# Seven products for eight in the MLP of a two-layer cross-attention kernel, with the last half's finished quarter stored first

## The chip, the core and the metric

The kernel runs on one core of one Trainium2 chip. The metric is the device time of one execution in microseconds (us), as a median over runs. All data are 4-byte floats. A core has TensorE (PE: matmuls, with its weight loads shown as PEld), VectorE (DVE), ScalarE (ACT), GpSimd (POOL) and SyncE (SP), which here only issues transfers. Each engine works through its own queue in order, and semaphores tie the queues together.

## The reference

Inputs are `x` (8 batches, 100 queries, 512 features) and a context (8, 361, 512). A first small cross-attention adds to `x`. Then comes one decoder layer with two cross-attentions of 16 heads of 128 (the context is key and value of both) and an MLP with 2048 hidden values. The change concerns the MLP alone:

```python
h = _layer_norm(x, ln_mlp_scale, ln_mlp_offset)
h = jax.nn.gelu(h @ w_fc1 + b_fc1, approximate=False) @ w_fc2 + b_fc2
return x + h
```

With 800 queries it is a product 800 x 512 x 2048 and one of 800 x 2048 x 512.

## The kernel before

Activations stand transposed: features on the 128 partitions, queries along the free dimension. The MLP is done in two halves (`hf` 0 and 1) of four batches, 400 queries each. A half has these units, built by `mlp_units`:

- `norm`: eight units `normed(2, q, c)` that normalise (L536) and transpose (`ph`, L542) into `hT`, 4 chunks of 128 features by 400 queries (L545).
- `hid`: sixteen units `hidden(hf, f)`, one for each 128 hidden values: four matmuls of 128x400 into one PSUM tile `pg` (L895), summed over the four feature chunks, and a Gelu with bias on ScalarE (L898) into `g`. The first eight go to a tile of their own, the others to a piece of the big constant tile `Z`, free by then.
- `mlp`: four units `mlp_out(hf, c)`, one for each 128 outputs: sixteen matmuls of 128x400 into `pf` (L907) over the hidden chunks, and an Identity with bias (L908) into `ys`, another piece of `Z`.
- `end`: four units `back`, one for each batch: four transposes into `pb` (L878), an add to the residual `xs` on VectorE (L879) and the store to `out` on the SP queue (L911).

Weights arrive through a ring of six slots of 512 KB (`W_SLOTS`, `Ring`). `emit` walks the list of units in order; when the last use of a tile is emitted, the fetch of the tile six places on is emitted too, on SP (L140). The framework adds the semaphores: a fetch waits for the last reader of its slot. The first layer's tiles hold 512 features by 256 hidden values, the second's 1024 hidden values by 128 outputs.

The order of the units is written out by hand at the end of the kernel; `woven` spreads one list over another. The framework's scheduler may then move an instruction a few places within its engine's queue. The last part of the order is:

```python
units += held[9:] + norm[:4] + woven(drain, norm[4:])
units += hid + woven(mlp, norm1) + woven(hid1, end) + mlp1 + end1
```

`drain` is the rest of the last attention, with its output projection `pwo` (L871: matmuls of 128x200). So in time: first half's hidden values, its outputs among the second half's transposes, second half's hidden values among the first half's ends, second half's outputs, its ends.

Other parts of the kernel already form seven products in place of eight: blocks of scores (`pair_part`, with sums from `pair_sums` on GpSimd, L668 to L671) and of probabilities times context (`mixed`, L795, with sums from `column_sums` on GpSimd, L759 to L762). There a partial result is copied or added out of a PSUM bank while the bank goes on accumulating, so that three banks `x`, `y`, `z` make four output blocks. In the first attention, `ctx_transposed` forms sums on VectorE (L423 to L425) while `ctx_sums` does so on GpSimd (L398 to L402).

Of the kernel before, what the change touches and what calls it, by code (L numbers as in the profile page):

```python
# [9 lines left out]
F32 = mybir.dt.float32  # L10
AF = mybir.ActivationFunctionType
ALU = mybir.AluOpType
# [27 lines left out]
B11, B21, B22, T1, T2, T3, T4 = range(7)  # L40


A11, A12, A22, A13, A23, A33, M1, M2, M3, M4 = range(10)
# [36 lines left out]
def two_cross_attentions(ctx: ExitStack, tc: tile.TileContext, a: dict, out: bass.AP):  # L80
    nc = tc.nc
# [11 lines left out]
    def psum(pool, shape, name):  # L93
        return pool.tile(shape, F32, tag=pool.name, name=name)
# [81 lines left out]
    def w4(key):  # L176
        return rings["w"].tiles[key].rearrange("p (c n) -> p c n", c=DT)

    def w8(key):
        return rings["w"].tiles[key].rearrange("p (h n) -> p h n", h=8)  # L180
# [5 lines left out]
    units = []  # L186

    def unit(fn, *keys):
        return fn, keys

    def emit():
        for _, keys in units:
            for ring, key in keys:
                rings[ring].plan(key)
        for ring in rings.values():
            ring.issue()
        for fn, keys in units:
            fn()
            for ring, key in keys:
                rings[ring].used(key)  # L200
                rings[ring].issue()
# [5 lines left out]
    zf = Z.rearrange("p c b r -> p (c b r)")  # L207
# [39 lines left out]
    vec_b = const.tile([P, len(VB), DT], F32, tag="vec_b", name="vec_b")  # L247
    vec = {v: vecs[:, i, :] for i, v in enumerate(VA + VC)}
# [7 lines left out]
    half = const.tile([L, 1], F32, tag="half", name="half")  # L256
# [264 lines left out]
    hTs = {}  # L521

    def normed(n, q, c):
        if c == 0:
            if n < 2:
                hTs[n, q] = work.tile([P, DT, NQ], F32, tag="hT", name=f"hT_{n}_{q}", bufs=1)
            elif q % 2 == 0:
                t = cpool.tile([P, 7 * 2 * KH], F32, tag="cT", name=f"hT_{n}_{q}")
                t = t[:, : DT * 2 * NQ].rearrange("p (c n) -> p c n", c=DT)
                for i in range(2):  # L530
                    hTs[n, q + i] = t[:, :, i * NQ : (i + 1) * NQ]
                hTs["mlp", q // 2] = t
            for j in range(QB):
                b = q * QB + j
                h = work.tile([L, D], F32, tag="h", name=f"h_{n}_{b}")
                nc.vector.tensor_scalar(  # L536
                    h, xs[b], mv[:, b, 0:1], rstd[:, b : b + 1], ALU.subtract, ALU.mult
                )
                hTs["rows", j] = h
        pt = psum(ps_t, [P, NQ], f"ph_{n}_{q}_{c}")  # L540
        for j in range(QB):
            nc.tensor.transpose(  # L542
                pt[:, j * L : (j + 1) * L], hTs["rows", j][:, c * P : (c + 1) * P], ident[:L, :L]
            )
        nc.vector.tensor_scalar(  # L545
            hTs[n, q][:, c, :], pt, vec_b[:, 2 * n, c : c + 1], vec_b[:, 2 * n + 1, c : c + 1], ALU.mult, ALU.add
        )
# [101 lines left out]
    pTs, probs, sums = {}, {}, {}  # L649
# [213 lines left out]
    ys = {}  # L863
# [7 lines left out]
            nc.tensor.matmul(ps, w[:, h % 8, :], oTs[l, q][:, h, :], start=(h == 0), stop=(h == H - 1))  # L871
        nc.scalar.activation(ys[l, q][:, c, :], ps, AF.Identity, bias=vec_b[:, 6 + l, c : c + 1])

    def back(y, off, b, then):

        ps = psum(ps_t, [L, D], f"pb_{b}")
        for c in range(DT):
            nc.tensor.transpose(ps[:, c * P : (c + 1) * P], y[:, c, off : off + L], ident)  # L878
        nc.vector.tensor_tensor(xs[b], ps, xs[b], ALU.add)  # L879
        then(b)  # L880


    gs = {}

    def hidden(hf, f):
        if f % 8 == 0:
            if f == 0:
                t = opool.tile([P, 8, 2 * NQ], F32, tag="o", name=f"g_{hf}_{f}")
            else:
                t = zf[:, (2 + hf) * 3200 : (3 + hf) * 3200].rearrange("p (f t) -> p f t", f=8)  # L890
            gs[hf, f // 8] = t
        w = w4(("f1", hf, f // 2))
        ps = psum(ps_mm, [P, 2 * NQ], f"pg_{hf}_{f}")
        for c in range(DT):
            nc.tensor.matmul(  # L895
                ps, w[:, c, (f % 2) * P : (f % 2 + 1) * P], hTs["mlp", hf][:, c, :], start=(c == 0), stop=(c == DT - 1)
            )
        nc.scalar.activation(gs[hf, f // 8][:, f % 8, :], ps, AF.Gelu, bias=vec["b_fc1"][:, f : f + 1])  # L898

    def mlp_out(hf, c):  # L900
        if c == 0:
            n = DT * 2 * NQ
            ys["mlp", hf] = zf[:, hf * n : (hf + 1) * n].rearrange("p (c t) -> p c t", c=DT)
        ps = psum(ps_mm, [P, 2 * NQ], f"pf_{hf}_{c}")
        for f in range(16):
            w = w8(("f2", hf, c, f // 8))
            nc.tensor.matmul(ps, w[:, f % 8, :], gs[hf, f // 8][:, f % 8, :], start=(f == 0), stop=(f == 15))  # L907
        nc.scalar.activation(ys["mlp", hf][:, c, :], ps, AF.Identity, bias=vec_b[:, 8, c : c + 1])  # L908

    def store(b):  # L910
        nc.sync.dma_start(out=out[b], in_=xs[b])  # L911
# [2 lines left out]
    W = "w"  # L914
# [41 lines left out]
    def close_units(l, q):  # L956
        res = [
            unit(lambda c=c: attn_out(l, q, c), (W, ("wo", l, q, c, 0)), (W, ("wo", l, q, c, 1)))
            for c in range(DT)
        ]  # L960
        res += [unit(lambda j=j: back(ys[l, q], j * L, q * QB + j, ln_stats)) for j in range(QB)]
        return res

    def mlp_units(hf):
        norm = [unit(lambda q=q, c=c: normed(2, q, c)) for q in (2 * hf, 2 * hf + 1) for c in range(DT)]
        hid = [unit(lambda f=f: hidden(hf, f), (W, ("f1", hf, f // 2))) for f in range(F // P)]
        mlp = [
            unit(lambda c=c: mlp_out(hf, c), (W, ("f2", hf, c, 0)), (W, ("f2", hf, c, 1))) for c in range(DT)
        ]
        end = [unit(lambda j=j: back(ys["mlp", hf], j * L, hf * 4 + j, store)) for j in range(4)]  # L970
        return norm, hid, mlp, end

    def woven(x, y):

        if not x:
            return y
        res, k = [], 0
        for n, u in enumerate(x):
            res.append(u)
            upto = (n + 1) * len(y) // len(x)  # L980
            res += y[k:upto]
            k = upto
        return res
# [37 lines left out]
    for n, (l, q, g) in enumerate(steps):  # L1021
        ahead = project_units(n + 1) if n + 1 < len(steps) else []
        half_ahead = (len(ahead) + 1) // 2
        for j in range(QB):
            fill = []
            if j == 0 and n and g == 1 and (l, q) != (0, 0):
                pl, pq, _ = steps[n - 2]
                fill += close_units(pl, pq)
            mix = mix_units(n, 0) if j else mix_units(n - 1, 1) if n else []
            part = ahead[:half_ahead] if j == 0 else ahead[half_ahead:]  # L1030
# [7 lines left out]
            part = woven(part, outs) if len(part) > len(outs) else woven(outs, part)  # L1038
            if mix:
                lead = (len(part) + 2) // 3 if ahead else len(part) - 2 + j  # L1040
                fill += part[:lead]
                part = part[lead:]
# [3 lines left out]
            if l == 0 and q == 1:  # L1046
                k = 2 * g + j
                fill += e_units(1)[4 * k // 3 : 4 * (k + 1) // 3]
            groups = score_units(n, j)
            k = 0  # L1050
            for i, us in enumerate(groups):
# [3 lines left out]
                k = upto  # L1055
    n = len(steps) - 1
    drain = mix_units(n, 1) + out_units(n) + close_units(1, B // QB - 1)
    norm, hid, mlp, end = mlp_units(0)
    norm1, hid1, mlp1, end1 = mlp_units(1)
    units += held[9:] + norm[:4] + woven(drain, norm[4:])  # L1060
    units += hid + woven(mlp, norm1) + woven(hid1, end) + mlp1 + end1
    emit()


# [23 lines left out]
```

## Time and profile before

| | us |
|---|---|
| median of 3 runs | 2073.28 (2072.14 to 2075.76) |
| the profiled execution | 2074.07 |
| its span | 2072.3 |
| TensorE busy (share of the span) | 2014.7 (97%) |
| VectorE, ScalarE, GpSimd busy | 1165.6, 748.5, 575.7 |
| pg (L895), first half | 1888 to 1931 |
| pf (L907), first half, with the second half's transposes | 1931 to 1975.5 |
| pg, second half, with the first half's ends | 1975.5 to 2020.3 |
| pf, second half | 2020.3 to 2063.3 |
| from there to the end of the span | 9.0 |

The span is the program on the chip in the profile; the time of an execution has some 1.8 us more around it. "Busy" is the union of an engine's instructions. The profile shows a 4-byte matmul as two records, each with a weight load of its own; their ends are modelled and overlap the next record, so the distance between starts says what one costs. Slices are fortieths of the span, 51.8 us each. The chain of waits is followed back from the last instruction, at each step to what released it.

### The profile page before, as it was taken

Reading aid. Unit: us, or ns where it says so; the run is one execution under the profiler, and the core shown is the slowest. Engines: PE = TensorE matmul, PEld = TensorE weight load, DVE = VectorE, ACT = ScalarE, POOL = GpSimd, SP = SyncE. Lnnn points to the kernel's source line nnn. Section 1 sums busy time; section 2 is a strip of 40 time slices with the busy share of each in tenths; the row PEclk is TensorE's granted clock in tenths of the full one; section 3 lists DMA queues with packets and bytes.
Section 4 is the critical chain, followed back from the end, with each engine's and each line's share of the span. In section 5 each row is a group of like instructions: output and inputs, shape, how many; then the busy total and the mean of one; then the engine's idle time right before and its main releaser. Section 6 shows DMA issues by size and latency. Waiting matters only on the chain. (4 is left out here: it accounts for less than half of the span.)

```text
span 2072.3 us, 30186 instructions
## 1 busy us (share of the span) xinstructions
PE 2014.7 (97%) x10735; PEld 1770.9 (85%) x10735; DVE 1165.6 (56%) x3363; ACT 748.5 (36%) x1962; POOL 575.7 (28%) x1042
## 2 busy tenths in 40 slices
PE   9989999999999999999999999999999999989998
PEld 5768899898899989998998999989998999877554
DVE  2564776657764766476645766476647574750000
ACT  1224544434343444244433443344334442421110
POOL 3332442323242234223232333233322322310000
PEclk9999999999999999999999999999999999999999
DMA  8784235442444134414442344234332433113331
GB/s 259 261 300 133 89 85 177 124 150 81 133 147 144 65 103 147 142 45 134 154 145 93 103 137 126 93 89 149 109 111 77 153 105 115 50 54 123 100 103 50
DMA packets 254109, 256.87 MB, mean 124 GB/s; under 512 B 35756, under 2 KB 226640, under 8 KB 250632
## 3 DMA queue, kind: packets, MB, share of 16 engines
q1 hardware_dynamic: 249776, 244.58, 37.0%
q0 software_dynamic: 2112, 6.40, 0.9%
q10 hardware_dynamic: 2072, 3.97, 0.6%
q8 instruction: 85, 1.39, 0.3%
q14 instruction: 64, 0.52, 0.1%
HBM read 229.24 MB, written 25.67 MB: 123 GB/s over the span
## 5 line engine op out<-in xcount | busy, mean ns | idle before, releaser
L331 DVE STREAM_TRANSPOSE pT<-p 32x192 f32<-32x192 f32 (+1 forms) x1664 | 602.2, 362 | 85.0 <-ACT p L315 57.1
L795 PE MATMUL mx<-pT,ctx 128*128 128x256 f32 (+3 forms) x960 | 282.7, 393 | 12.9 <-DVE Z L821 5.5
L685 PE MATMUL sx<-cT,Z 128*128 128x181 f32 x1152 | 229.4, 318 | 4.8 <-DVE p L725 4.8
L795 PE MATMUL mz<-pT,ctx 105*128 105x256 f32 (+3 forms) x768 | 209.8, 396 | 11.2 <-POOL pT L759 9.4
L685 PEld LDWEIGHTS sx<-cT,Z 128*128 128x128 f32 x1152 | 195.7, 191 | 18.5 <-DVE p L725 6.8
L795 PEld LDWEIGHTS mx<-pT,ctx 128*128 128x128 f32 (+1 forms) x960 | 169.9, 190 | 35.4 <-POOL pT L761 8.0
L641 PE MATMUL pqw<-q,wkT 128*128 128x200 f32 x1024 | 195.8, 333 | 0.0
L625 PE MATMUL pq<-hT,wq 128*128 128x200 f32 x1024 | 194.0, 333 | 1.7 <-DMA wq<-in_L_xattn_wq_dram 1.7
L847 PE MATMUL po<-Z,wv 128*128 128x200 f32 x1024 | 193.9, 333 | 0.6 <-DMA wv<-in_L_xattn_wv_dram 0.6
L795 PEld LDWEIGHTS mz<-pT,ctx 128*128 128x128 f32 (+1 forms) x768 | 145.4, 193 | 46.0 <-POOL pT L759 12.8
L641 PEld LDWEIGHTS pqw<-q,wkT 128*128 128x128 f32 x1024 | 177.2, 190 | 5.4 <-ACT p L315 0.3
L625 PEld LDWEIGHTS pq<-hT,wq 128*128 128x128 f32 x1024 | 175.0, 189 | 7.4 <-issue 2.0
L719 POOL TENSOR_SCALAR p<-nsb 128x1 f32<-128x1 f32 x192 | 33.3, 193 | 526.3 <-DVE pT L331 481.8
L847 PEld LDWEIGHTS po<-Z,wv 128*128 128x128 f32 x1024 | 174.8, 189 | 5.2 <-issue 1.6
L739 ACT ACTIVATE p<-p,nm 128x362 f32<-128x362 f32 x192 | 114.8, 598 | 169.2 <-DVE nm L738 167.5
L871 PE MATMUL pwo<-oT,wo 128*128 128x200 f32 x1024 | 175.8, 332 | 0.0
L871 PEld LDWEIGHTS pwo<-oT,wo 128*128 128x128 f32 x1024 | 173.2, 190 | 0.0
L668 POOL TENSOR_TENSOR sums<-Z 128x256 f32<-128x256 f32 x96 | 69.9, 728 | 324.2 <-ACT Z L644 188.8
L738 DVE TENSOR_REDUCE nm<-p 128x1 f32<-128x362 f32 x192 | 101.5, 529 | 99.0 <-ACT p L730 87.4
L685 PE MATMUL sz<-cT,sums 128*128 128x181 f32 x768 | 150.6, 318 | 0.4 <-ACT p L713 0.4
L644 ACT COPY Z<-pqw 128x400 f32<-128x400 f32 x256 | 122.9, 489 | 74.3 <-PE pqw L641 74.1
L315 ACT ACTIVATE p<-p,rden 128x362 f32<-128x362 f32 (+2 forms) x216 | 129.6, 600 | 31.0 <-DVE rden L314 30.9
(310 smaller groups left out, 2720.7 us busy)
## 6 DMA issues: line engine op xcount, KB each, us to landing
wv<-in_L_xattn_wv_dram SPq DMA_DIRECT2D x64, 512.0 KB
wq<-in_L_xattn_wq_dram SPq DMA_DIRECT2D x64, 512.0 KB
wo<-in_L_xattn_wo_dram SPq DMA_DIRECT2D x64, 512.0 KB
wkT<-wkd SPq DMA_DIRECT2D x48, 512.0 KB
cT<-cTd SPq DMA_DIRECT2D x16, 1267.0 KB
f<-in_L_xattn_w_fc_dram SPq DMA_DIRECT2D x32, 512.0 KB
wkr<-in_L_xattn_wk_dram SPq DMA_DIRECT2D x16, 512.0 KB
ctx<-cxd SPq DMA_DIRECT2D x16, 512.0 KB
```

Of the source, the lines that this page charges most:

```text
L315: nc.scalar.mul(p[:rows, :n], p[:rows, :n], rden[:rows])
L331: nc.vector.transpose(dst[keys, :, :, i, :], src[i * QD : (i + 1) * QD, :, :, quarter, :])
L625: nc.tensor.matmul(ps, w[:, c, (h % 2) * K : (h % 2 + 1) * K], hTs[l, q][:, c, :], start=(c == 0), stop=(c == DT - 1),)
L641: nc.tensor.matmul(ps[:, c, :], w[:, h % 2, cc * P : (cc + 1) * P], qs[h], start=True, stop=True)
L644: nc.scalar.copy(Z[:, 2 * c2 : 2 * c2 + 2, :, h * L : (h + 1) * L], ps.rearrange("p c (b t) -> p c b t", b=QB),)
L668: nc.gpsimd.tensor_tensor(t[:, 0], a2[:, :2, :], a2[:, 2:, :], ALU.add)
L685: nc.tensor.matmul(ps[:, :KH], st["a"][a][:, c, :], st["ct"][:, blk, c, :], start=(first and c == 0), stop=(c == 1), skip_group_check=not ...
L738: nc.vector.tensor_reduce(nm, p[:, :S1], AX.X, ALU.max, negate=True)
L739: nc.scalar.activation(p[:, :S1], p[:, :S1], AF.Exp, bias=nm, accum_out=den)
L795: nc.tensor.matmul(ps, cx[:w, blk, :], pT[:w, u, :], start=first, stop=last, skip_group_check=more)
L847: nc.tensor.matmul(ps, w[:, c, (h % 2) * K : (h % 2 + 1) * K], Z[:, c, :, h * L : (h + 1) * L], start=(c == 0), stop=(c == DT - 1),)
L871: nc.tensor.matmul(ps, w[:, h % 8, :], oTs[l, q][:, h, :], start=(h == 0), stop=(h == H - 1))
```

## The change

Both MLP products are done in blocks: outputs in two rows of blocks, inputs (the contraction) in two, and the 400 queries in two columns of 200 (a quarter of all queries each). Four output blocks then take seven block products in place of eight. Sums of weight blocks (S1, S2, S3, S4) and of value blocks (T1 to T4) are formed first; S3 and T3 replace a block in place.

- `hidden_in` forms the input's T sums on VectorE. `hidden_sums` forms the first layer's weight sums for a block of 256 hidden values from each of two tiles (`k` and `4 + k`) on GpSimd. `hidden` has four parts per block; its seven products are four matmuls of 128x200 each. Results are copied out on ScalarE, completed by an add on VectorE, and given their Gelu in place (A22 T4's directly from PSUM). At the end of a block VectorE forms the T sums of the hidden values.
- `mlp_sums` forms the second layer's weight sums for two outputs chunks (`c`, `c + 2`) on VectorE, and `mlp_out` has four parts with seven products of eight matmuls of 128x200.
- `left_sums` and `right_sums` are the sums' formulas. `g`'s second tile and the T sums now have one place in `Z` for both halves, where each half had its own.
- `back` can do its transposes in two goes. The batches `j` = 2 and 3 of a half, whose outputs lie in the blocks c12 and c22, end first; in the second half they are put inside the last product (`between`, after its fourth matmul), and of batches 0 and 1 three transposes stand ahead of the last.
- Weights are fetched in the new order of use; a tile pair is held for the whole of its block.

```diff
@@ -871,41 +871,145 @@
             nc.tensor.matmul(ps, w[:, h % 8, :], oTs[l, q][:, h, :], start=(h == 0), stop=(h == H - 1))
         nc.scalar.activation(ys[l, q][:, c, :], ps, AF.Identity, bias=vec_b[:, 6 + l, c : c + 1])
-    def back(y, off, b, then):
-
-        ps = psum(ps_t, [L, D], f"pb_{b}")
-        for c in range(DT):
+    pbacks = {}
+    def back(y, off, b, then, chunks=range(DT)):
+        if b not in pbacks:
+            pbacks[b] = psum(ps_t, [L, D], f"pb_{b}")
+        ps = pbacks[b]
+        for c in chunks:
             nc.tensor.transpose(ps[:, c * P : (c + 1) * P], y[:, c, off : off + L], ident)
+        if DT - 1 not in chunks:
+            return
+        del pbacks[b]
         nc.vector.tensor_tensor(xs[b], ps, xs[b], ALU.add)
         then(b)
...
+    gs, ts, ws, mm = {}, {}, {}, {}
+    def right_sums(engine, b11, b12, b21, b22, t1, t2, t4):
+        engine.tensor_tensor(t1, b12, b11, ALU.subtract)
+        engine.tensor_tensor(t2, b22, t1, ALU.subtract)
+        engine.tensor_tensor(b12, b12, b22, ALU.subtract)
+        engine.tensor_tensor(t4, b21, t2, ALU.subtract)
+    def left_sums(engine, a11, a12, a21, a22, s1, s2, s4):
+        engine.tensor_tensor(s1, a21, a22, ALU.add)
+        engine.tensor_tensor(s2, s1, a11, ALU.subtract)
+        engine.tensor_tensor(s4, a12, s2, ALU.subtract)
+        engine.tensor_tensor(a21, a21, a11, ALU.subtract)
+    def blocks_of(t, n):
+        return [t[:, i * n : (i + 1) * n, j * NQ : (j + 1) * NQ] for i in range(2) for j in range(2)]
+    def hidden_in(hf):
+        h = blocks_of(hTs["mlp", hf], 2)
+        t = work.tile([P, 3, 2, NQ], F32, tag="pb", name=f"ht_{hf}", bufs=1)
+        right_sums(nc.vector, *h, t[:, 0], t[:, 1], t[:, 2])
+        ts["h", hf] = dict(zip(("B11", "T3", "B21", "B22", "T1", "T2", "T4"), h + [t[:, i] for i in range(3)]))
+        g0 = opool.tile([P, 8, 2 * NQ], F32, tag="o", name=f"g_{hf}")
+        g1 = zf[:, 3200:6400].rearrange("p (f t) -> p f t", f=8)
+        t = zf[:, 6400:11200].rearrange("p (u f t) -> p u f t", u=3, f=8)
+        g = [x[:, :, j * NQ : (j + 1) * NQ] for x in (g0, g1) for j in range(2)]
+        gs[hf] = g
+        ts["g", hf] = dict(zip(("B11", "T3", "B21", "B22", "T1", "T2", "T4"), g + [t[:, i] for i in range(3)]))
+    def hidden_sums(hf, k):
+        w1, w2 = w4(("f1", hf, k)), w4(("f1", hf, 4 + k))
+        t = work.tile([P, 3, 2, 256], F32, tag="pT", name=f"fs_{hf}_{k}")
+        blocks = [w1[:, :2], w1[:, 2:], w2[:, :2], w2[:, 2:]]
+        left_sums(nc.gpsimd, *blocks, t[:, 0], t[:, 1], t[:, 2])
+        ws["h", hf, k] = dict(zip(("A11", "A12", "S3", "A22", "S1", "S2", "S4"), blocks + [t[:, i] for i in range(3)]))
+    def hidden(hf, k, part):
+        a, b = ws["h", hf, k], ts["h", hf]
+        c11, c12, c21, c22 = (g[:, 2 * k : 2 * k + 2, :] for g in gs[hf])
+        key = "h", hf, k
+        def add(name, sa, sb, first=False):
+            if first:
+                mm[key, name] = psum(ps_mm, [P, 2, NQ], f"p{name}_{hf}_{k}")
+            ps = mm[key, name]
+            for f in range(2):
+                for c in range(2):
+                    nc.tensor.matmul(
+                        ps[:, f, :], a[sa][:, c, f * P : (f + 1) * P], b[sb][:, c, :],
+                        start=first and f == c == 0, stop=f == c == 1, skip_group_check=True,
+                    )
+            return ps
+        def gelu(dst, src, block):
+            for f in range(2):
+                i = block * 8 + 2 * k + f
+                nc.scalar.activation(dst[:, f, :], src[:, f, :], AF.Gelu, bias=vec["b_fc1"][:, i : i + 1])
+        if part == 0:
+            nc.scalar.copy(c11, add("gx", "A11", "B11", True))
+            nc.vector.tensor_tensor(c11, add("gy", "A12", "B21", True), c11, ALU.add)
+            gelu(c11, c11, 0)
+        elif part == 1:
+            nc.scalar.copy(c22, add("gz", "S1", "T1", True))
+            nc.scalar.copy(c12, add("gx", "S2", "T2"))
+        elif part == 2:
+            nc.vector.tensor_tensor(c12, add("gz", "S4", "B22"), c12, ALU.add)
+            gelu(c12, c12, 0)
+            nc.vector.tensor_tensor(c22, add("gx", "S3", "T3"), c22, ALU.add)
+            gelu(c22, c22, 1)
+        else:
+            gelu(c21, add("gx", "A22", "T4"), 1)
+            t = [ts["g", hf][n][:, 2 * k : 2 * k + 2, :] for n in ("T1", "T2", "T4")]
+            right_sums(nc.vector, c11, c12, c21, c22, *t)
+    def mlp_sums(hf, c):
+        blocks = [w8(("f2", hf, cc, half)) for cc in (c, c + 2) for half in range(2)]
+        t = cpool.tile([P, 20 * P], F32, tag="ctx", name=f"fs1_{hf}_{c}")
+        t = t[:, :2048].rearrange("p (u f n) -> p u f n", u=2, f=8)
+        s4 = work.tile([P, 8, P], F32, tag="pT", name=f"fs4_{hf}_{c}")
+        left_sums(nc.vector, *blocks, t[:, 0], t[:, 1], s4)
+        ws["o", hf, c] = dict(zip(("A11", "A12", "S3", "A22", "S1", "S2", "S4"), blocks + [t[:, 0], t[:, 1], s4]))
+    def mlp_out(hf, c, part, between=lambda: None):
+        if (c, part) == (0, 0):
             n = DT * 2 * NQ
             ys["mlp", hf] = zf[:, hf * n : (hf + 1) * n].rearrange("p (c t) -> p c t", c=DT)
...
+        a, b = ws["o", hf, c], ts["g", hf]
+        c11, c12, c21, c22 = (ys["mlp", hf][:, cc, j * NQ : (j + 1) * NQ] for cc in (c, c + 2) for j in range(2))
+        key = "o", hf, c
+        def add(name, sa, sb, first=False):
+            if first:
+                mm[key, name] = psum(ps_mm, [P, NQ], f"p{name}_{hf}_{c}")
+            ps = mm[key, name]
+            for f in range(8):
+                nc.tensor.matmul(
+                    ps, a[sa][:, f, :], b[sb][:, f, :],
+                    start=first and f == 0, stop=f == 7, skip_group_check=True,
+                )
+                if f == 3:
+                    between()
+            return ps
+        def biased(dst, ps, cc):
+            nc.scalar.activation(dst, ps, AF.Identity, bias=vec_b[:, 8, cc : cc + 1])
+        if part == 0:
+            biased(c11, add("fx", "A11", "B11", True), c)
+            nc.vector.tensor_tensor(c11, add("fy", "A12", "B21", True), c11, ALU.add)
+        elif part == 1:
+            biased(c22, add("fz", "S1", "T1", True), c + 2)
+            biased(c12, add("fx", "S2", "T2"), c)
+        elif part == 2:
+            nc.vector.tensor_tensor(c12, add("fz", "S4", "B22"), c12, ALU.add)
+            nc.vector.tensor_tensor(c22, add("fx", "S3", "T3"), c22, ALU.add)
+        else:
+            biased(c21, add("fx", "A22", "T4"), c + 2)
     def store(b):
         nc.sync.dma_start(out=out[b], in_=xs[b])
@@ -963,11 +1067,21 @@
     def mlp_units(hf):
         norm = [unit(lambda q=q, c=c: normed(2, q, c)) for q in (2 * hf, 2 * hf + 1) for c in range(DT)]
-        hid = [unit(lambda f=f: hidden(hf, f), (W, ("f1", hf, f // 2))) for f in range(F // P)]
-        mlp = [
-            unit(lambda c=c: mlp_out(hf, c), (W, ("f2", hf, c, 0)), (W, ("f2", hf, c, 1))) for c in range(DT)
-        ]
-        end = [unit(lambda j=j: back(ys["mlp", hf], j * L, hf * 4 + j, store)) for j in range(4)]
+        hid, mlp = [unit(lambda: hidden_in(hf))], []
+        for k in range(4):
+            keys = [(W, ("f1", hf, k)), (W, ("f1", hf, 4 + k))]
+            sums = unit(lambda k=k: hidden_sums(hf, k), *keys)
+            hid.insert(len(hid) - 2 if k else 0, sums)
+            hid += [unit(lambda k=k, part=part: hidden(hf, k, part), *keys) for part in range(4)]
+        for c in range(2):
+            a11, a12, a21, a22 = ((W, ("f2", hf, cc, half)) for cc in (c, c + 2) for half in range(2))
+            mlp.insert(len(mlp) - 1 if c else 0, unit(lambda c=c: mlp_sums(hf, c), a11, a12, a21, a22))
+            for part, keys in enumerate(((a11, a12), (), (a21,), (a22,))):
+                mlp.append(unit(lambda c=c, part=part: mlp_out(hf, c, part), *keys))
+        def ends(j, chunks=range(DT)):
+            return unit(lambda: back(ys["mlp", hf], j * L, hf * 4 + j, store, chunks))
+        end = [ends(2), ends(3)] + [ends(j, cs) for cs in (range(3), range(3, 4)) for j in range(2)]
         return norm, hid, mlp, end
     def woven(x, y):
@@ -1058,7 +1172,13 @@
     norm, hid, mlp, end = mlp_units(0)
     norm1, hid1, mlp1, end1 = mlp_units(1)
     units += held[9:] + norm[:4] + woven(drain, norm[4:])
-    units += hid + woven(mlp, norm1) + woven(hid1, end) + mlp1 + end1
+    def whole():
+        for fn, _ in end1[:2]:
+            fn()
+    mlp1[-1] = unit(lambda: mlp_out(1, 1, 3, whole), *mlp1[-1][1])
+    units += hid + woven(mlp, norm1) + woven(hid1, end) + mlp1 + end1[2:]
     emit()
 
```

More of the change, by code (lines that the diff above doesn't have):

```diff
@@ L879, in back @@
         nc.vector.tensor_tensor(xs[b], ps, xs[b], ALU.add)
         then(b)
[L883 to L898, printed above, removed]
@@ L900, in mlp_out @@
-    def mlp_out(hf, c):
-        if c == 0:
+    gs, ts, ws, mm = {}, {}, {}, {}
[9 more added lines that the diff above has]
+        engine.tensor_tensor(a21, a21, a11, ALU.subtract)
@@ L902, in mlp_out @@
+    def mlp_out(hf, c, part, between=lambda: None):
+        if (c, part) == (0, 0):
             n = DT * 2 * NQ
             ys["mlp", hf] = zf[:, hf * n : (hf + 1) * n].rearrange("p (c t) -> p c t", c=DT)
[L904 to L908, printed above, removed]
+        a, b = ws["o", hf, c], ts["g", hf]
[26 more added lines that the diff above has]
+            biased(c21, add("fx", "A22", "T4"), c + 2)
```

## The prediction

> **What bounds the kernel now.** First the engines' busy time, then the slices, then the chain of waits through the last 210 us. TensorE is busy for 97% of the span, and the last six or so slices are the MLP:
>
> ```profile
> PE 2014.7 (97%) x10735; PEld 1770.9 (85%) x10735; DVE 1165.6 (56%) x3363; ACT 748.5 (36%) x1962; POOL 575.7 (28%) x1042
> ...
> PE   9989999999999999999999999999999999989998
> ...
> DVE  2564776657764766476645766476647574750000
> ACT  1224544434343444244433443344334442421110
> POOL 3332442323242234223232333233322322310000
> PEclk9999999999999999999999999999999999999999
> ```
>
> Read the right end: there VectorE and GpSimd are near zero and ScalarE is at one tenth, while TensorE stays full and its clock is granted. So in the MLP only the count of TensorE passes sets the time, and three engines stand free. The chain of waits says the same stretch by stretch (start, length, engine, tile, records):
>
> ```profile
> 1870.71 16.27 PE pwo L871 x96
> 1886.98 1.05 PE pb L878 x8
> 1888.21 43.01 PE pg L895 x128
> 1931.22 10.75 PE pf L907 x32
> ...
> 2020.43 42.99 PE pf L907 x128
> 2063.42 0.66 PE pb L878 x6
> 2065.07 0.68 DVE x L879
> 2065.75 0.60 DVEq L1084
> 2066.35 0.60 DVE x L879
> ```
>
> No wait lies between pg and pf. A product in the code is two records here (L895's 128 products of both halves stand as 256). So a product with 400 columns costs 42.99/64 = 0.672 us, and one with 200 columns (pwo) 16.27/48 = 0.339 us. Two narrow ones cost 0.678: splitting the queries costs 1%.
>
> **What the Trainium skill says.** "TensorE: Matmul & The Clock Gate", section Back-to-back issue gap: the spacing of a stream is set by weight load and matmul together. The trace agrees and tells which one rules: weight loads of 190 ns overlap, since pwo's records, each with its load, follow each other every 169.5 ns. More loads per column are thus already inside 0.339. "GPSIMD Engine Reference", section Elementwise — side-by-side cycle accounting, gives GpSimd about 2.6 cycles per element for two inputs at 1.2 GHz (2.17 ns); the trace's rows L759 to L762, 128x256 in about 734 ns and 128x288 in about 795, give 2 ns per element. The same page, section Specifications, says that GpSimd shares its SBUF interface with a VectorE instruction that has two SBUF inputs. The trace shows it, alone and beside GpSimd:
>
> ```profile
> 107.34 0.54 DVE L423 TENSOR_TENSOR cT_-1_5_736<-cT_-1_5_736 128x362 f32<-128x362 f32 x1
> 107.39 1.08 POOL L400 TENSOR_TENSOR msum<-ctx_-1_4_557 128x256 f32<-128x256 f32 x1
> ...
> 108.78 1.05 DVE L425 TENSOR_TENSOR cT_-1_5_736<-cT_-1_5_736 128x362 f32<-128x362 f32 x1
> ```
>
> VectorE 0.54 grows to 1.05, GpSimd 0.73 to 1.08. "ScalarE: Activation LUTs", section Table sets: the hidden batching unit: copy and identity are in every set. The trace has one load of 1.28 us (L898) for Gelu and Identity in turn; I count no new load.
>
> **The change part by part.**
>
> *Products.* Removed: 128 in `hidden` and 128 in `mlp_out`, 256 x 0.672 = 172.0 us. Added: per half, 4 blocks of 7 x 4 in `hidden` and 2 of 7 x 8 in `mlp_out`, together 448 of 200 columns: 448 x 0.339 = 151.9. On the path: **-20.1 us**.
>
> *Weight sums of the first layer* (`hidden_sums`, GpSimd): 4 of 128x512 per block. 730 + 256 x 2.1 = 1.27 us each, 5.1 per block, 7.5 if all collide with VectorE. A block of 28 products takes 9.5 us. The first two sums have their tiles early: the SP issues at 1873.5, 1876.2, 1878.9 and 1881.6 each land some 3.5 us later, so sums 0 and 1 end near 1884.5 and 1890; block 0 starts near 1888 and S1 is wanted four to five products in. Behind them on GpSimd stand two rstd (L339), wanted 30 us later. Hidden by TensorE: 0.
>
> *Weight ring.* Six slots hold three blocks' pairs instead of six tiles of two units. The last reader of a pair's second tile is A22 T4, some 2.4 us into the next block; the fetch lands 3.5 us later, the sums take 5.1, and it is wanted 23 us after release. The SP queue is strict: the stores of x_148 and x_149 come before one fetch, those of x_146 and x_147 before another; their adds are done when the slots behind them come free. 0.
>
> *Sums over hidden values and evacuations.* Per block VectorE has three adds from PSUM (128x256 417 ns, 128x288 about 450, so 0.57 at 400) and four sums (0.58: the 362-element row's 0.537 plus 38 x 1.04), 4.0 us, 6 with collisions. ScalarE has three copies (L644: 0.489), two gelus from PSUM (0.43) and six from SBUF (0.46), 5.1. Both are under 9.5, so only hand-offs matter. The tightest: S3 T3 ends, VectorE adds c22 (0.2 + 0.57 + 0.05), then A22 T4 may write the same bank, 0.82 and up to 0.19 of exposed weight load. The built order puts three products of the next block between (1.02): just enough. Where it puts four transposes and one product (second half, block 0) it lacks 0.2; between the quarters of `mlp_out` about 0.1, before the very last product 0.2. At the start S4 B22 waits for a copy and S2 T2 for another: 0.4.
>
> *Weight sums of the second layer* (`mlp_sums`, VectorE): 4 of 128x1024, 1.22 us each (L374: 1600 in 1.824, slope 1.04), four times. In VectorE's queue three of them stand ahead of block 3's c12 and c22 adds. They wait for a fetch released 2.4 us into block 3, landing at 5.9, ending at 9.6; the adds then end at 10.8 where A22 T4 would start at 10.5: about 0.5 lost in the first half; in the second, five products cover it. Stalls in all: **+1.5**, estimated; ends 0 and 6 (below nothing they cannot go: the chain of before has no idle there to win).
>
> *Start.* T1 to T4 of the input (four x 0.58) wait for hT's last chunk, 1890.8 before; T2 is then ready near 1892, wanted near 1893.5. 0.
>
> *Transposes and end.* The first half's 16 transposes, four adds and four stores are the same and only reordered within the second half's products: 0. Of the second half's 16 transposes into pb, 8 move ahead of or into the last product: 8 x 0.109 = **+0.9**. After the last product stood ScalarE 0.595, four adds at 0.60 apart, and 5.3 us from the last store's issue at 2066.98 to the end. Now the copy is 0.43 and two adds follow instead of four, -1.2 - 0.15; with two stores gone ahead the last one lands perhaps 0.25 sooner (the third landed in 3.5, the fourth in 4.0). **-1.6**.
>
> Sum: -20.1 + 1.5 + 0.9 - 1.6 = -19.3. The profiled execution took 2074.07 (span 2072.3 and 1.8 around it): 2054.8. The median of the runs shown is 0.8 below it: **2054.0**, span about 2053.
>
> **The rivals.**
>
> *Hand-offs bite.* Every block pays about 1 us because a collision on SBUF pushes VectorE past its 1.02 cover, and each quarter set of the second layer 0.5: 8 + 2 instead of 1.5, about 2062.5. For it: covers are within 0.1 us of need. Against: GpSimd works only half of a block.
>
> *Narrow groups cost more.* If in groups of four the weight load's 190 ns ruled each record, 448 x 0.38 = 170.2, only 1.8 gained on the products: 2072. The unbroken pwo and po rows speak against it (32 records of po at L847 in 5.42 us: the same 0.339). This is the case in which seven for eight does not pay.
>
> *GpSimd becomes the bound, slower than before.* If a 512-wide sum took 3.3 us, the four would need 13.2 per block, 3.7 over, times 8 = 29.6 lost: about 2084. It loses from (9.5 + 19.3/8)/4 = 3.0 us per sum on. Against: the slope gives 1.27, the worst collision 1.9.
>
> **How the numbers follow.** Forecast 0.85; hand-offs 0.09, also faster; narrow groups 0.03; GpSimd bound or another stall over 19 us 0.03. Measurement tells about 0.2% (4 us) from nothing. Faster 0.94, same 0.03, slower 0.03. The range: no stall and a better end give 2052 and 0.8 for the runs' scatter 2051; six us of stalls give 2058.5, so 2051 to 2059.
>
> **What would show it.** Right: between pwo and the end the TensorE records of L942 and L991 in steps of 0.34 per product, some 152 us in all; VectorE and GpSimd no longer zero in the last slices; 128x512 sums on GpSimd near 1.3 us; two adds behind the last product. Wrong: idle of the weight load on VectorE ahead of pgx or on GpSimd ahead of pgz over 5 us in sum, a second table load, or a pitch near 0.38.

## The result, and the profile after

| | before, us | after, us |
|---|---|---|
| median of 4 runs each, same chip | 2074.52 (2072.14 to 2076.34) | 2056.78 (2053.21 to 2061.5) |
| the profiled execution | 2074.07 | 2053.21 |
| its span | 2072.3 | 2051.4 |
| start of the MLP stretch | 1888.05 | 1885.32 |
| MLP stretch | 175.38 | 159.90 |
| tail | 8.84 | 6.19 |

The kernel became faster by 17.7 us: after to before is 0.9917, 95% interval 0.9892 to 0.9941. The last three rows cut the span in three. The *MLP stretch* runs from the first TensorE record into pg (pgx after the change) to the end of the last one into pf (pfx), and the *tail* from there to the end of the span. These two are used for every experiment below, for the following reason.

The spans differ by 20.85 us, but 2.73 of it lies ahead of the MLP, where the change touches nothing. There TensorE's granted clock drops to half in windows of 3.4 us. Before the MLP the execution of before has 20.5 us of half clock, that of after 13.6, and a second profiled execution of after had 27.3 and entered the MLP at 1892.89. So 6.8 us of half clock cost 2.73 us and 13.6 us cost 7.57: some 1.4 to 1.9 us for each window. How many windows an execution has differs from run to run, and in the first comparison the spans of after's four runs follow their mean clock: 2051.4 at 0.996, 2053.6 at 0.995, 2056.4 at 0.994 and 2059.7 at 0.993. The windows aren't the whole scatter: of three kernels below whose executions had 17.05 us of half clock there, two entered the MLP at 1886.2 and 1886.4, the third at 1889.8. What the change itself is worth is the stretch, -15.48, and the tail, -2.65: **-18.1 us**.

The page of after, engines and slices. Each digit is the busy tenth of one fortieth of the span:

```profile
PE 1994.6 (97%) x11119; PEld 1822.8 (89%) x11119; DVE 1227.6 (60%) x3455; ACT 766.9 (37%) x2026; POOL 617.9 (30%) x1074
...
PE   9998999999999999999999999999999999989998
...
DVE  2564776647764766466664757476647664772543
ACT  1224544424342444334433444344433442421331
POOL 3332442323242242323332332232233232323140
PEclk9999999999999999999999999999999999999999
```

TensorE has 384 more records (448 x 2 less 256 x 2) and 20.1 us less of busy time. The right end of VectorE's row, four zeros before, now reads 2543, ScalarE's reads 1331 for 1110, and GpSimd works until the last slice but one. PE's own row hardly differs: work of 62 us on VectorE, 42 on GpSimd and 18 on ScalarE was taken into the shadow of TensorE.

The chain of waits of after (start, length, engine, tile, line, records), at the places shown of before:

```profile
1867.99 16.27 PE pwo L871 x96
1884.26 1.05 PE pb L882 x8
...
1966.47 1.35 PE pgy L942 x8
...
2019.76 8.17 PE pfx L991 x48
...
2043.87 1.35 PE pfx L991 x8
2045.22 0.85 PE pb L882 x7
...
2046.10 0.69 DVE x L886
2046.79 0.60 DVEq L1204
```

A product of 200 columns (two records) costs 1.35/4 = 0.338 in a group of four and 8.17/24 = 0.340 in a long run, the same as pwo's 16.27/48 = 0.339. What stood as four unbroken blocks now stands as many short ones. Most follow each other without a gap; the waits between 1885 and 2045.3 name those that don't (engine, tile and line, what it waited for; total us, times, longest):

```profile
PEld pgx L942 <- DVE Z L963: 2.2, 3, 1.1
...
PE pgx L942 <- DVE Z L963: 1.3, 2, 0.8
...
PEld pgz L942 <- issue: 1.0, 2, 0.8
...
PE pgz L942 <- ACT Z L958: 0.5, 1, 0.5
```

The weight load waits first and the matmul with it, so the rows overlap and aren't added. Read from the starts of TensorE's records, the stretch has 3.75 us of gaps: 0.80 and 1.06 at A22 T4 of block 3 in the first and the second half (a product goes by its weight block and its value block; `pgx` behind L963; in each, 0.10 stands behind the product's first record and not ahead of it), 0.69 at S4 B22 of the first half's block 2 (`pgz` behind L958), 0.40 at the start, and 0.8 in crumbs of 0.07 to 0.2.

The gap of 0.69 was in no step of the prediction. Its story is in the timeline of after (start, length, engine, line, operation; in brackets the idle time before it and what ended it):

```profile
1904.04 1.29 DVE L896 TENSOR_TENSOR Z<-g 128x400 f32<-128x400 f32 x1
1905.44 1.46 DVE L897 TENSOR_TENSOR Z<-Z 128x400 f32<-128x400 f32 x1
1906.82 1.65 DVE L898 TENSOR_TENSOR g<-g,Z 128x400 f32<-128x400 f32 x1
1908.39 0.56 DVE L899 TENSOR_TENSOR Z<-Z 128x400 f32<-128x400 f32 x1
1908.88 0.56 DVE L955 TENSOR_TENSOR g<-pgy,g 128x400 f32<-128x400 f32 x1
...
1904.85 1.61 POOL L905 TENSOR_TENSOR f<-f,f 128x512 f32<-128x512 f32 x1
1906.42 1.61 POOL L904 TENSOR_TENSOR fs<-f,fs 128x512 f32<-128x512 f32 x1
...
1909.47 0.81 ACT L951 ACTIVATE g<-g,vecs 128x200 f32<-128x200 f32 x2 [2.42 <-DVE g L955]
1910.19 0.47 ACT L958 COPY Z<-pgz 128x400 f32<-128x400 f32 x1
```

Three T sums of block 1 take 4.4 us in place of 1.7 while GpSimd forms weight sums. The fourth, with GpSimd done, is back at 0.56. In VectorE's queue behind them stands block 2's add to c11 (L955), in ScalarE's behind that add stands c11's Gelu (L951), and behind the Gelu the copy of pgz out of its bank (L958). S4 B22 accumulates into that bank and starts only at 1910.80. Four engines in order carry one slow sum to TensorE.

The wait of 1.06 in the second half, on VectorE's timeline:

```profile
2000.52 1.23 DVE L902 TENSOR_TENSOR fs<-f,f 128x1024 f32<-128x1024 f32 x1 [1.07 <-DMA f<-in_L_xattn_w_fc_dram]
2001.78 1.23 DVE L903 TENSOR_TENSOR fs<-fs,f 128x1024 f32<-128x1024 f32 x1
2002.92 1.22 DVE L905 TENSOR_TENSOR f<-f,f 128x1024 f32<-128x1024 f32 x1
2004.06 0.57 DVE L961 TENSOR_TENSOR g<-pgz,g 128x400 f32<-128x400 f32 x1
2004.54 1.22 DVE L904 TENSOR_TENSOR fs<-f,fs 128x1024 f32<-128x1024 f32 x1
2005.67 0.57 DVE L963 TENSOR_TENSOR Z<-pgx,Z 128x400 f32<-128x400 f32 x1
```

All four of `mlp_sums`' sums stand ahead of c22's add (L963), on whose bank A22 T4 waits; TensorE could have started it at 2005.3, and started it at 2006.30. In the first half the fourth sum (L904) comes after that add.

### The profile page after: what moved, and what is told of

Same layout as the page of the kernel before. It is cut to its first block, busy times and chain, and to the rows that moved or that the text cites. A ratio compares the mean times of both kernels' runs of the same rounds, so it can differ in the third digit from the quotient of the medians.

```text
span 2051.4 us, 31244 instructions
## 1 busy us (share of the span) xinstructions
PE 1994.6 (97%) x11119; PEld 1822.8 (89%) x11119; DVE 1227.6 (60%) x3455; ACT 766.9 (37%) x2026; POOL 617.9 (30%) x1074
```

## The experiments

Single executions scatter by several us, so most experiments are read from one profiled execution by stretch and tail, not by its whole time. The stretches of after's two executions differ by 0.5, so a smaller difference says little. The theory under test: the products gain 20.1 us, and VectorE's order and its collisions with GpSimd give some 2.5 of it back. Rivals: GpSimd's work costs nothing that matters, or the tail's gain is chance.

### The old end

All transposes of the last half after its last product, as before the change:

```diff
...
-    mlp1[-1] = unit(lambda: mlp_out(1, 1, 3, whole), *mlp1[-1][1])
-    units += hid + woven(mlp, norm1) + woven(hid1, end) + mlp1 + end1[2:]
+    end1 = [
+        unit(lambda j=j: back(ys["mlp", 1], j * L, 4 + j, store)) for j in range(4)
+    ]
+    units += hid + woven(mlp, norm1) + woven(hid1, end) + mlp1 + end1
```

> The changed kernel with the second half's four ends whole behind the last product, in the order 0 to 3, as before the change. Measured are the MLP's stretch on TensorE (first pgx to the end of the last pfx; 159.90 us in the changed kernel, 175.38 before) and the tail behind it (6.19 and 8.84). Theory, the tail is paid for by the number of adds and stores left behind the last product: eight transposes of 0.109 us leave the stretch (159.0), the tail goes back to before's 8.84 less the 0.17 that the copy of 200 columns is shorter (8.7), the last store lands some 4.0 us after its issue; the sum gets 1.6 longer. Rival, the quick landing of the last store in the changed kernel (2.7 us where 4.0 was before) was chance: the last store lands in about 2.7 here too and the tail is 7.4.

Measured: 2055.97 us, stretch 159.74, tail 8.04. Its chain ends so:

```profile
2042.73 0.55 PE pb L882 x5
2043.27 2.89 PE pfx L991 x16
2046.16 0.56 PE pb L882 x5
...
2046.74 1.29 DVE x L886 x2
2048.03 0.60 DVEq L1202
2048.63 0.60 DVE x L886
```

The framework's scheduler drew five of the finished batches' transposes ahead of the last product by itself (first row), so the stretch didn't fall by the 0.9 of the transposes, and the tail is shorter than that of before. Stretch and tail together are 1.7 us worse than after's; 1.6 was expected. Four adds stand 0.6 us apart where after has two, and the last store takes 3.67 us from issue (2049.26) to landing with three others close ahead of it, where after's takes 2.73 (2047.42 to 2050.15) and before's took 4.0. The earlier stores are worth something in the landing itself, and chance doesn't explain it: the last store landed in 2.7 us in all eight executions with the new end and in 3.7 to 4.0 in the three with the old one. The tails of after, 6.19 and 6.15, stayed at that size in every other kernel with the new end but the slowed one (6.17, 6.19, 6.21, 6.22, 6.20).

### The second layer's weight sums on GpSimd

```diff
-        left_sums(nc.vector, *blocks, t[:, 0], t[:, 1], s4)
+        left_sums(nc.gpsimd, *blocks, t[:, 0], t[:, 1], s4)
```

> The second layer's weight sums on GpSimd in place of VectorE. Theory, TensorE's two longest idle times (0.80 and 1.06 us ahead of the last block's A22 T4 in each half) come from VectorE's queue: three of these sums stand there ahead of block 3's c12 and c22 adds and wait for a fetch. Without them both idle times go and the stretch falls from 159.9 to about 158.1. Rival, the c22 add is late by itself, or the sums at GpSimd's 2 ns per element (2.3 us each, 9.4 for four) come too late for the S1 product: the stretch stays at 159.9 or grows by 2 or more, with idle ahead of pfz.

Measured: 2058.54 us, stretch 158.21, tail 6.17. The waits of this kernel for the same tiles:

```profile
PE pgz L942 <- ACT Z L958: 0.5, 1, 0.5
PEld pgx L942 <- DVE Z L963: 0.4, 2, 0.2
```

The row of pgx behind L963 falls from 2.2 us to 0.4, that of pgz behind L958 stays to the digit. So both gaps of block 3 came from VectorE's queue and not from the fetch of the weights, which this kernel awaits as well, on GpSimd.

### No weight sums on GpSimd after block 0

Blocks 1 to 3 of each half use block 0's sums S1, S2 and S4, and their S3 is the plain block. Their hidden values are therefore others; the products are as many.

```diff
...
+        if k:
+            names = "A11", "A12", "S3", "A22"
+            ws["h", hf, k] = {**ws["h", hf, 0], **dict(zip(names, blocks))}
+            return
```

> GpSimd's weight sums are made for block 0 of each half alone; the other blocks use block 0's S1, S2, S4 and the plain third weight block for S3, with the same fetches and products, so that the output is not the reference's. Theory, VectorE's sums of hidden values (L896 to L898, 0.87 to 0.97 us in the mean, up to 1.65) are long because they collide with GpSimd's sums on SBUF: they fall to about 0.58 each, the adds and copies behind them are on time, and the idle 0.69 us ahead of S4 B22 in block 2 of the first half goes; the two idle times of about 0.9 at the blocks 3 stay. Stretch about 159.1. Rival, these sums are long by their own operands (two rows of 200 out of rows of 400): they stay at 0.9 and the idle time stays.

Measured: 2056.22 us, stretch 158.43, tail 6.19. The groups of the T sums (line, engine, operation, count; busy us, mean ns; idle before), in after:

```profile
L898 DVE TENSOR_TENSOR g<-g,Z 128x400 f32<-128x400 f32 x8 | 7.8, 971 | 0.0
...
L897 DVE TENSOR_TENSOR Z<-Z 128x400 f32<-128x400 f32 x8 | 7.6, 956 | 1.5 <-ACT Z L951 1.2
```

and in this kernel:

```profile
L897 DVE TENSOR_TENSOR Z<-Z 128x400 f32<-128x400 f32 x8 | 4.6, 573 | 2.1 <-ACT Z L955 2.0
L898 DVE TENSOR_TENSOR g<-g,Z 128x400 f32<-128x400 f32 x8 | 4.5, 568 | 0.0
```

Without GpSimd's sums the same instruction takes 0.57 us. The gap at block 2 is gone, and those at block 3 are still there (0.73 and 0.93 where after has 0.80 and 1.06). The T sums' own operands, the rival here, aren't what makes them long. The two causes are separate: this kernel takes away the one, the one before it the other.

### GpSimd's sums more than doubled

Three of the four sums are formed three times over, ten instructions per block in place of four, with the same values:

```diff
+        for _ in range(2):
+            nc.gpsimd.tensor_tensor(t[:, 0], blocks[2], blocks[3], ALU.add)
+            nc.gpsimd.tensor_tensor(t[:, 1], t[:, 0], blocks[0], ALU.subtract)
+            nc.gpsimd.tensor_tensor(t[:, 2], blocks[1], t[:, 1], ALU.subtract)
         left_sums(nc.gpsimd, *blocks, t[:, 0], t[:, 1], t[:, 2])
```

> The same kernel with S1, S2 and S4 of the first layer's weights made three times over: ten GpSimd sums per block in place of four. Theory, GpSimd has slack up to a block's 9.5 us of products and becomes the bound beyond it: ten at 1.36 are 13.6 per block. From the landing of the tiles on, the sums of the blocks 0 to 3 of the first half are then ready at 4, 17, 31 and 45 us after the stretch's start, the last of them 14 us late; in the second half the first two are in time and the last 5 us late. Stretch about 179, with the idle time ahead of pgz. Rival, what the changed kernel loses at present is GpSimd's rate already, so that six more sums cost their full 8.2 us in each of eight blocks: stretch 220 or more. Rival, GpSimd is far from mattering: under 162.

Measured: 2080.52 us beside 2078.64 for an execution of before, stretch 181.53, tail 6.47. Its waits, its timeline at the three longest of them, and its busy times by stretch (us; PE, PEld, DVE, ACT and POOL with counts; PEclk, DMA share, GB/s):

```profile
PEld pgz L946 <- POOL fs L902: 10.4, 4, 4.7
...
PE pgz L946 <- POOL fs L902: 9.2, 4, 4.4
```

```profile
1921.93 2.36 PE L946 MATMUL pgz<-ht,fs 128*128 128x200 f32 x8 [4.37 <-POOL fs L902]
...
1935.63 2.41 PE L946 MATMUL pgz<-ht,fs 128*128 128x200 f32 x8 [2.28 <-POOL fs L902]
...
2027.06 1.70 PE L946 MATMUL pgz<-hT,fs 128*128 128x200 f32 x8 [2.15 <-POOL fs L904]
```

```profile
1917.50:1922.00 4.50, 0.13 (x2) 0.07 (x1) 2.51 (x3) 0.81 (x2) 4.26 (x5) 1.00 0.38 111
1922.00:1926.00 4.00, 4.00 (x14) 4.00 (x15) 0.00 (x0) 0.49 (x1) 4.00 (x4) 0.58 0.00 0
1926.00:1936.00 10.00, 7.72 (x45) 7.42 (x45) 7.14 (x7) 3.25 (x8) 9.61 (x8) 1.00 0.37 106
```

TensorE now waits for GpSimd itself, and GpSimd is busy throughout (4.26 of 4.5, 4.00 of 4.0, 9.61 of 10). Here the prediction's losing rival holds: ten sums of 1.34 to 1.68 us in the mean don't fit under a block's 28 products of 9.5 us, four do. Three half-clock windows stood inside this stretch, at 1922.65, 1936.31 and 2028.47, each 0.7 to 1.4 us behind the end of one of the three waits shown. No other execution has a window in its MLP stretch. At 1.4 to 1.9 us each they cost some 5 us by estimate, so 181.53 measures both, and some 176 would stand against the 179 expected, which was without them.

### One layer alone

The first layer's product in blocks, the second as before the change, with the old end and without the hidden values' T sums:

```diff
...
-            t = [ts["g", hf][n][:, 2 * k : 2 * k + 2, :] for n in ("T1", "T2", "T4")]
-            right_sums(nc.vector, c11, c12, c21, c22, *t)
...
+        mlp = [
+            unit(lambda c=c: mlp_out(hf, c), (W, ("f2", hf, c, 0)), (W, ("f2", hf, c, 1))) for c in range(DT)
+        ]
```

> The first MLP product in seven for eight, the second and the ends as before the change. Theory (each part pays by its count of products, and the idle times belong to the meeting of the two): 224 x 0.339 for 128 x 0.672 is -10.1 us; no sums of hidden values and no second-layer weight sums stand in VectorE's queue, so the idle times of 0.69 in block 2 and of 0.80 and 1.06 in the blocks 3 are gone; about 0.8 of small ones stay. Stretch 166.1 where it was 175.38, tail 8.8. Rival (the first product's own hand-offs idle TensorE): the three idle times stay, stretch 168.5.

Measured: 2062.78 us, stretch 166.18, tail 8.68.

The second layer's alone, with the new end, the hidden values as before the change and their T sums formed once all four blocks stand:

```diff
...
+        if f > 8 and f % 2:
+            k = (f - 8) // 2
...
             right_sums(nc.vector, c11, c12, c21, c22, *t)
...
-        hid, mlp = [unit(lambda: hidden_in(hf))], []
...
+        hid = [unit(lambda f=f: hidden(hf, f), (W, ("f1", hf, f // 2))) for f in range(F // P)]
```

> The second MLP product in seven for eight, with the sums of hidden values it needs and the earlier stores; the first product as before the change. Theory: -10.1 us for the products, +0.9 for eight transposes that come ahead of the end, 0.3 idle between quarters; the second-layer weight sums ahead in VectorE's queue delay nothing, since the first product leaves VectorE nothing on TensorE's path. Stretch 166.5, tail 6.2. Rival (the second product waits for its weight sums or for the sums of hidden values): idle ahead of pfz of over 2 us, stretch over 168.5.

Measured: 2064.3 us, stretch 166.37, tail 6.21.

Each layer's products are worth 10.05 us by the pitch. The first layer alone shortens the stretch by 9.20, the second by 9.01, in which the eight transposes moved into the stretch count as +0.9. Together that is 18.2, and the whole change has 15.5 (16.0 in its second execution, further down). The missing 2.2 to 2.7 us are lost only where the layers meet: `mlp_sums` in VectorE's queue during `hidden`, and the hidden values' T sums beside GpSimd's weight sums. Neither kernel has both.

### Both causes taken away

The second layer's sums on GpSimd, and c11's Gelu no longer ahead of the copies in ScalarE's queue. It runs later, together with c12's, on 400 columns at once:

```diff
...
-            gelu(c11, c11, 0)
...
-            gelu(c12, c12, 0)
+            g = g0s[hf][:, 2 * k : 2 * k + 2, :]
+            gelu(g, g, 0)
...
-        left_sums(nc.vector, *blocks, t[:, 0], t[:, 1], s4)
+        left_sums(nc.gpsimd, *blocks, t[:, 0], t[:, 1], s4)
```

> The changed kernel with two edits: the second layer's weight sums on GpSimd, and the Gelu of c11 taken together with c12's, in two instructions of 400 columns behind c12's add, so that ScalarE's copies of pgz and pgx never stand behind a Gelu that waits for VectorE. Theory: the waits at the ends of the blocks 3 and the 0.69 us ahead of S4 B22 both go; stretch 157.4 (no idle at all would be 175.38 - 20.1 + 0.9 = 156.2). Rival: the collision only moves on, to VectorE's c12 and c22 adds, and the wait comes back ahead of A22 T4: 158.2 or more, as with the weight sums moved alone. The whole time should fall by 2 to 3 us against the changed kernel, some 0.9% under the kernel before; that is less than its runs scatter, so the stretch decides.

Measured, 4 runs: 2056.41 us (2053.2 to 2059.19), beside 2077.41 (2071.8 to 2078.41, 7 runs) of before; ratio 0.9908, interval 0.9889 to 0.9927. Stretch 157.39, tail 6.22. No matmul into pg waits for anything any more, and of the weight loads' waits this is the largest:

```profile
PEld pgx L943 <- DVE Z L964: 0.4, 2, 0.2
```

T sums and weight sums still collide, and longer than in after: beside sums of 128x1024 two of block 3's T sums took 2.54 and 2.73 us. Nobody stands behind them now who matters. This kernel and the one with the second layer's sums on GpSimd differ in the Gelu alone, and that one still had the gap at S4 B22. So the collision reached TensorE through the Gelu's place in ScalarE's queue.

### After and this version, side by side

Both on one chip in five rounds, with nine runs of before between them.

> The changed kernel once more, in five rounds beside the kernel before. Theory: what the change is worth is the difference of the stretch and the tail, 15.5 + 2.65 = 18.1 us, and the rest of the differences between single executions comes from stretches of half clock elsewhere in the kernel; the medians differ by 18.1 give or take 2, ratio 0.9913. Rival: the first comparison's 17.7 hides a gain or loss ahead of the MLP, where two executions were 2.7 us apart: 15.5 or 20.9.

Measured: 2057.59 us (2056.52 to 2060.27), before 2073.61 (2070.53 to 2076.45); ratio 0.9926, interval 0.9914 to 0.9939. Stretch 159.42, tail 6.15.

> The kernel with the second layer's weight sums on GpSimd and the joint Gelu of c11 and c12, in five rounds. Theory: its stretch is 2.5 us shorter than the changed kernel's (157.4 against 159.9), so the medians differ by about 2.5, ratio to the kernel before 0.990. Rival: the scatter of the runs (some 8 us from the lowest to the highest) covers it, and the two medians lie within 1.5 of each other in either order.

Measured: 2054.35 us (2051.49 to 2056.93); ratio 0.9907, interval 0.9892 to 0.9921. Stretch 157.40, tail 6.20.

The change measures 16.0 us here, 17.7 in the first comparison and 18.1 from the traces. Expected were 18.1 give or take 2 and a ratio of 0.9913. What was measured falls just short of both, and 16.0 is nearer to the rival's 15.5, which means a loss ahead of the MLP. The traces show no such loss, though they can't exclude one of 1 to 2 us: with the same 20.5 us of half clock, before entered the MLP at 1888.05 and the version with both causes taken away at 1887.79 and 1889.63. The version with both causes taken away is 3.2 us better by the medians and 2.0 to 2.5 by the stretches, which agree to 0.01 between its two executions and to 0.5 between after's. The intervals of the two ratios overlap, so the step is shown by the traces rather than by the times. It is the best of the kernels run.

## Why the prediction was right, and where its sizes were off

| step | predicted, us | measured, us | from |
|---|---|---|---|
| products | -20.1 | -20.1 | stretch less gaps and transposes; pitch 0.338 to 0.340 |
| stalls | +1.5 | +3.75 | gaps between TensorE's records |
| transposes moved | +0.9 | +0.9 | eight more inside the stretch |
| tail | -1.6 | -2.65 | 8.84 to 6.19 |
| sum | -19.3 | -18.1 | |

**Products.** Right, and with them the rival of narrow groups fell: a group of four costs no more per product than an unbroken run. The one-layer kernels show the gain split in nearly equal halves, 9.2 and 9.9 without the transposes.

**Weight sums on GpSimd.** Put at 1.27 us, 1.9 in the worst collision; measured 1.27 to 1.29 on average for those that ran mostly alone (L902, L903 in after), 1.42 to 1.46 for L904 and L905, 1.61 in the worst. They stayed hidden, and the kernel with ten of them shows both that the rival of GpSimd as the bound is a real mechanism and that the kernel isn't there. The weight ring cost nothing on its own either: GpSimd's waits for fetches never reached TensorE.

**Stalls.** This is the step that failed in size, in two terms. First, "in the second, five products cover it". That was worked out with three sums ahead of c22's add, as in the first half. The five products did stand there (`pfx`, ten records from 2003.64). But in the second half all four sums stand ahead of the add, 1.22 us more, and 1.06 were lost. The first half's term, 0.5, measured 0.80. The kernel with these sums on GpSimd shows the cause of both. Second, the collisions were budgeted as a total per block ("6 with collisions", with the remark that only hand-offs matter), and the tightest hand-off was looked for behind S3 T3 alone. The T sums' means over eight blocks, 568 to 971 ns, are inside that budget. What was overlooked is what is queued behind them: an add, a Gelu and a copy on two engines, to a bank that TensorE needs. The kernel without GpSimd's sums shows the collision as the root, the one with the later Gelu the way it travels. The start's 0.4 came out as 0.40.

The rival of hand-offs that bite named this very mechanism, a collision pushing VectorE past its cover. It priced it at about 1 us for every block, 10 in all. It bit in one block of eight. Three T sums collide in a row in two more blocks, 0 and 1 of the second half (1.26, 1.04 and 1.64 us; 1.29, 1.46 and 1.64). Behind the latter S4 B22 again starts 6.75 us after the first of them, at 1991.16. But TensorE had six transposes more to do by then, some 0.65 us, and only 0.1 was lost. That cover wasn't tried by an experiment.

**Tail.** Two adds fewer and the shorter copy came as put (1.35). The last store's landing was put at 0.25 sooner and came 1.3 sooner (4.0 to 2.73). The old end with the new products has 3.67 there, so most of it is the two stores gone ahead.

The two errors of size nearly cancel: +2.25 and -1.05 leave 1.2 us between -19.3 and -18.1. The rest of the way to the median of 2056.78 is scatter between executions, the clock windows among it; it isn't worked out further. Had the tail not been mis-sized the other way, the stalls would have shown more plainly.

## What to carry to other kernels

When free engines are given work under the one that is the bound, the sum of their busy time says little: list for every slow or collidable instruction what stands behind it in its own queue, follow that to the next engine's queue, and do it for each half or block whose order differs. A sum that feeds the next stage doesn't belong on the engine that returns banks to TensorE if another has room. A difference of a few us at 2000 is better read from the stage that the change touches than from the whole time.

## What the runs showed of the hardware that was not expected

- A VectorE sum of two SBUF operands of 128x400 took 0.57 us without GpSimd's sums beside it, up to 1.71 beside those of 128x512, and up to 2.73 beside those of 128x1024. The pair in the trace of before had shown twice (0.54 to 1.05). But it is no factor, and the first of that pair was not alone, as the prediction reads it: GpSimd's sum (L400) began 0.05 us after it, and it kept its 0.54. All twelve long ones in after's MLP stretch ended 0.43 us after the end of the GpSimd sum that was running when they began, and so (0.43 to 0.44) in the kernel with both causes taken away:

```profile
1929.28 2.68 POOL L904 TENSOR_TENSOR fs<-f,fs 128x1024 f32<-128x1024 f32 x1
1929.67 2.73 DVE L898 TENSOR_TENSOR g<-g,Z 128x400 f32<-128x400 f32 x1
```

  It looks as if the sum stood until GpSimd's instruction ended, so that what it loses is what is left of that instruction. VectorE's adds with one operand in PSUM (to c12 and c22) kept 0.57 beside such sums. Whether shorter GpSimd instructions would help was not tried. GpSimd lost less: its sums went from 1.27 to 1.61 in after, and those of 128x1024 from 2.35 to 2.68.
- TensorE's clock halves in windows of 3.41 us (some of 6.83), four to seven of them ahead of the MLP, at 1.4 to 1.9 us each by the two differences worked out above. They stand behind TensorE's waits. In the eleven traces 61 windows begin before the end of TensorE's work: 49 of them within 5.1 us of the start of a wait of 1.88 us or more, the other twelve behind two shorter waits close together (0.82 and 0.92, or 1.03 and 1.38). The two waits below, shown from before, stand in every execution, and a window follows each in all eleven:

```profile
1816.16 0.88 PE L685 MATMUL sx<-cT,Z 128*128 128x181 f32 x4 [2.29 <-DVE p L725]
...
1844.52 2.08 PE L795 MATMUL mz<-pT,ctx 128*128 128x256 f32 x4 [3.84 <-POOL pT L759]
```

  Of the 58 waits of that length nine have no window behind them, and the wait of 1.81 us at 1904.23 in the kernel with ten sums has none either. That is a connection in time: waits were added to a quiet stretch once, in that kernel, and three windows came with them; none was taken away. If it holds, an idle TensorE costs more than its idle time.
- A store of 200 KB landed 2.7 us after its issue with one other close ahead of it (eight executions), and 3.7 to 4.0 with three (three executions).
